# First adjacency over SyncE's and GpSimd's queues, weights folded at earlier steps, the first norm's steps reordered

## The chip, the core and the metric

The kernel runs on one core of one Trainium2 chip. The metric is device time in microseconds (us) of the whole launch; TensorE is PE, VectorE is DVE, ScalarE is ACT, GpSimd is POOL, and SyncE (SP) issues DMAs.

## The reference, cut to what matters

For each of 16 samples there are 1024 nodes of 128 features, `x`, and a weighted adjacency `adj` of 1024 x 1024, all float32.

```python
# stage 0
degree = adj.sum(-1)[:, :, None]
agg = einsum('bid,bij->bjd', x, adj) / degree
x = layernorm(x + relu(concat([x, agg]) @ W.T + b))
# stage 1: four layers; the inputs of the last two are widened by earlier layers
src_agg = einsum('bjv,bij->biv', nodes @ ws + bs, adj / l2norm(adj, rows))
dst_agg = einsum('bjv,bji->biv', nodes @ wd + bd, adj / l2norm(adj, columns))
nodes = tanh(concat([src_agg, nodes @ wn + bn, dst_agg]) @ wu + bu)
# at the end
x = layernorm(x + nodes)
```

## The kernel before, in words

The weights of a layer are folded once (`fold_begin`, `fold_end`, lines 139 to 165): `ws`, `wd` and `wn` are transposed on PE and multiplied by their parts of `wu`, so that a layer needs one product for messages (`pt`, line 484) and one for a node's own part. Folded weights of layers one to three are written to memory (`wsave`, line 165) and fetched layer by layer. The unfolded weights lie in a buffer `raw` that the second sample's adjacency later takes.

The samples are worked one after the other. While a sample goes through its four layers, the adjacency of the next is loaded, squared and summed (`sums`, line 226), scaled and transposed in between. The first sample has no such cover, and its loading, stage 0 and first layer are written out by hand (lines 690 to 934). This is the part that the change touches, besides the last norm.

Adjacency is kept in 8 blocks of 128 rows, each put together from four groups of 32 partitions. `PAIRS` names four pairs of blocks; `load_pair` (line 697) loads one pair with four DMAs of 256 KB, one for each group; `load_nodes` loads half of the nodes. `load_rows` (line 429) loads a quarter of the adjacency once more in another layout, in 8 DMAs of 128 KB, from which DVE's 32 x 32 transposes make the transposed adjacency `at` (`transpose_rows`). Before that, ACT scales the rows by the inverse row norms `rinv` (`scale_rows`, line 438).

Stage 0 of the first sample: each block is squared on ACT (`square`), its degree is reduced on DVE (`degree`), its squares are added up on POOL (`add_square`, seven additions into one), and PE gathers it (`gather`, two matmuls a block). Then come the aggregate scaled by the inverse degree (`scaled`), the product with `W` (`first_weights`), the sum with `x` and the transposing back in PSUM (`with_x`, `with_y`), the norm (`norm_stats` takes statistics on DVE and the power of -0.5 on POOL; half 1 is written by ACT with a shift, half 0 by DVE), and `to_x1`, which transposes the result on PE for the first layer's messages. `row_inverses`, `column_sums` and `inverses` turn the sums of squares into scales.

The first layer is `plain_layer` (line 509): 34 PE steps, and at the steps named in `hooks` work of other engines is put into their queues: scaling of columns (`second0`, `first0`), transposing of rows (`rows0`), folding of the later layers' weights (`folded`), and `sums0`, which makes sums of quarters of the adjacency (`combine`, line 466) for the next layer. The later layers (`aggregate`, line 539) form their products from seven quarter products instead of eight, so they need these sums. Hooks do not set a time: every engine works through its own queue in the order written, and waits by semaphores.

An engine also issues its DMAs in that order. A wait on a DMA's queue holds all that stands behind it in the same engine's queue. The DMAs share eight semaphores in turn for SP and ACT, and eight for POOL, so that the ninth in flight waits until the first has landed.

Of the kernel before, what the change touches and what calls it, by code (L numbers as in the profile page):

```python
# [8 lines left out]
F32 = mybir.dt.float32  # L9
AF = mybir.ActivationFunctionType  # L10
ALU = mybir.AluOpType
# [12 lines left out]
def adj_resnorm_kernel(ctx: ExitStack, tc: tile.TileContext, x, adj, w0, b0, layers, out):  # L24
# [224 lines left out]
    def column_sums(b, state):  # L249

        tr = two.tile([P, N], F32, tag="sq", name=f"acct{b}")
        nc.vector.transpose(tr, state["acc"])
        part = two.tile([P, K], F32, tag="part", name=f"part{b}")
        nc.vector.reduce_sum(part, tr.rearrange("p (k r) -> p k r", r=C), axis=AX.X)
        state["part"] = part
# [113 lines left out]

    def norm_stats(pn, blks, name):  # L370

        n = len(blks)
        stats = one.tile([P, BPH, 6], F32, tag="stats", name=f"st{name}")
        mv = two.tile([P, BPH, 2], F32, tag="mv", name=f"mv{name}")
        for q in range(n):
            nc.vector.bn_stats(stats[:, q], pn[:, blks[q]])
            nc.vector.bn_aggr(mv[:, q], stats[:, q])
        ve = two.tile([P, BPH], F32, tag="ve", name=f"ve{name}")
        nc.vector.tensor_scalar_add(ve[:, :n], mv[:, :n, 1], LN_EPS)
        rstd = two.tile([P, BPH], F32, tag="rst", name=f"rs{name}")  # L380
        nc.gpsimd.tensor_tensor(rstd[:, :n], ve[:, :n], mhalf[:, :n], ALU.pow)
        return mv, rstd

    def norm_write(dst, pn, stats, q):
        mv, rstd = stats
        nc.vector.tensor_scalar(dst, pn, mv[:, q, 0:1], rstd[:, q:q + 1], op0=ALU.subtract, op1=ALU.mult)

    def norm_shift(stats, n, name):
        mv, rstd = stats
        shift = two.tile([P, BPH], F32, tag="shift", name=f"sh{name}")  # L390
        nc.vector.scalar_tensor_tensor(shift[:, :n], mv[:, :n, 0], -1.0, rstd[:, :n], op0=ALU.mult, op1=ALU.mult)
        return shift

    def norm_write_act(dst, pn, stats, shift, q):
        nc.scalar.activation(dst, pn, AF.Identity, bias=shift[:, q:q + 1], scale=stats[1][:, q:q + 1])

# [31 lines left out]

    def load_rows(b, q, st):


        v = adj[b, q * QB * C:(q + 1) * QB * C].rearrange("(k r) (h g j) -> h g r k j", r=C, h=NH, g=G)
        for g in range(G):
            for h in range(NH):
                nc.sync.dma_start(st[g * C:(g + 1) * C, :, h * P:(h + 1) * P], v[h, g])
        return st
# [260 lines left out]
    def load_pair(q, pair, groups):  # L697
        h, k = pair
        for g in groups:
            q.dma_start(a[g * C:(g + 1) * C, h * BPH + k:h * BPH + k + 2], av[h][g, :, k:k + 2])  # L700

    def load_nodes(h):
        for g in range(G):
            nc.sync.dma_start(xn[g * C:(g + 1) * C, h * BPH:(h + 1) * BPH], xv[h][g])

    load_pair(nc.scalar, PAIRS[0], range(G))
    load_nodes(1)
    load_pair(nc.scalar, PAIRS[1], range(2))
    load_pair(nc.sync, PAIRS[1], range(2, G))
    load_nodes(0)  # L710
    load_pair(nc.sync, PAIRS[2], range(G))
    nc.sync.dma_start(w0n, w0)
    nc.sync.dma_start(b0c, b0.rearrange("(p o) -> p o", o=1))
    load_pair(nc.sync, PAIRS[3], range(G))
    raw = Raw()
    wm = message_tile("wm1_0")
    fetched = [fetch_weights(raw, 0, nc.sync, wm)]
    Q = combined(0, "Q")
    rows = {q: load_rows(0, q, Q[i].rearrange("p k (u c) -> p (k u) c", u=2)) for i, q in ((2, 2), (3, 3))}
    fetched += [fetch_weights(raw, l, nc.sync) for l in range(1, NL)]  # L720
    rows[0] = load_rows(0, 0, Q[4].rearrange("p k (u c) -> p (k u) c", u=2))
    rows[1] = load_rows(0, 1, one.tile([P, 2 * NJ, HW // 2], F32, tag="T2", name="rows1_0"))

    make_identity(nc, ident)
    nc.vector.memset(mhalf, -0.5)
# [7 lines left out]
    xT = two.tile([P, N], F32, tag="xT", name="x0_T")  # L733
    for h in (1, 0):
        pt = product(f"xtr0_{h}")
        for q in range(BPH):
            nc.tensor.transpose(pt[:, q * P:(q + 1) * P], xn[:, h * BPH + q], ident)
        nc.scalar.copy(nodes(xT[:, half(h)]), blocks(pt))

    sq = []  # L740
# [25 lines left out]

    for h, k in PAIRS[:-1]:
        for i in range(h * BPH + k, h * BPH + k + 2):
            square(i)
            degree(i)  # L770
            if i != BPH:
                add_square(i)
            for h2 in (1, 0):
                gather(h2, i)
    pt = product("w0tr")
    for k in range(2):
# [33 lines left out]
    degree_row(1)  # L810
    with_x(1)
    with_x(0)
    first, second = 2, 3
# [5 lines left out]
    degree(first)  # L819
    scaled(1)  # L820
    degree(second)
    degree_inverses(0)
    add_square(first)
    nc.vector.tensor_scalar_max(cols[:, :NB], cols[:, :NB], NORM_EPS * NORM_EPS)
    nc.gpsimd.tensor_tensor(inv[:, :NB], cols[:, :NB], mhalf[:, :NB], ALU.pow)
    first_weights(0, 1, xT, agT, yT, blocks, nodes)
    degree_row(0)
    scaled(0)
    with_y(1)
    first_weights(0, 0, xT, agT, yT, blocks, nodes)  # L830
    stats = {1: norm_stats(pn[1], range(BPH), "0_0_1")}
    fold_begin(0, fetched[0], nc.vector.tensor_copy)
    with_y(0)
    fold_end(0, fetched[0])
    rinv = row_inverses(0, inv)
    shift = norm_shift(stats[1], BPH, "0_0_1")
    for q in range(BPH):
        norm_write_act(x1n[:, BPH + q], pn[1][:, q], stats[1], shift, q)
    stats[0] = norm_stats(pn[0], range(BPH), "0_0_0")
    add_square(second)  # L840
    to_x1(1)
    for q in range(BPH):
        norm_write(x1n[:, q], pn[0][:, q], stats[0], q)
    to_x1(0)

# [11 lines left out]
    for b in range(B):  # L857
# [9 lines left out]
        if b == 0:  # L867
            for q in (2, 3):
                scale_rows(rows[q], q, rinv)
            t = messages(b, 0, feats, wm, {0: lambda: column_sums(0, st0)}, with_sums=False)  # L870
            cinv = {}

# [10 lines left out]
            def second0(destination, finish):  # L883
                columns0(range(NJ, NB), 1)
                destination(1, cinv[0])
                columns0(range(NJ), 1)
                for q in (0, 1):
                    scale_rows(rows[q], q, rinv)
# [9 lines left out]
            def sums0(destination, finish):  # L898
                combine_1(y)
                finish(1)  # L900
                combine(2, y, T)
                combine_1(yt)

            def folded(l, part):
                return lambda *_: part(l, fetched[l])

            hooks = {1: lambda *_: inverses(0, st0, NB), 3: rows0, 5: folded(1, fold_begin), 7: cinv0,
                     9: folded(1, fold_end), 10: second0, 18: first0, 19: folded(2, fold_begin),
                     22: folded(2, fold_end), 24: folded(3, fold_begin), 26: sums0, 29: folded(3, fold_end)}
            T = combined(0, "T")  # L910
# [48 lines left out]
        def quarters2(b=b):  # L959
            if b == 0:  # L960
                combine(3, y, T)
                combine(2, yt, Q)
            for i in (3, 4):
                combine(i, yt, Q)
# [5 lines left out]
        if b == 0:  # L970
            hooks[20] = lambda: combine(4, y, T)
        aggregate(b, 1, feats, t, a, at, T, Q, f23, "acc", hooks)
# [104 lines left out]
        else:  # L1077
# [7 lines left out]
            def transpose_last():  # L1085
                pn["last"] = ps_t.tile([P, BPH, P], F32, tag="pt", name="on_1")
                for q in range(BPH):
                    i = BPH + q
                    nc.tensor.transpose(pn["last"][:, q], f4[:, i * P:(i + 1) * P], ident)
                stats[1] = norm_stats(pn["last"], range(BPH), f"1_{b}_1")  # L1090

# [22 lines left out]
    shift = norm_shift(stats[1], BPH, f"1_{b}_1")  # L1114
    for q in range(BPH):
        norm_write_act(o[:, BPH + q], pn["last"][:, q], stats[1], shift, q)
    nc.sync.dma_start(ov[:, BPH:], o[:, BPH:])
    for i in pieces:
        for q in range(2):
            nc.tensor.matmul(pn[i][:, q], f4[:, (i + q) * P:(i + q + 1) * P], ident, start=False, stop=q == 1)  # L1120
        stats[0] = norm_stats(pn[i], range(2), f"1_{b}_0_{i}")
        for q in range(2):
            norm_write(o[:, i + q], pn[i][:, q], stats[0], q)
        nc.sync.dma_start(ov[:, i:i + 2], o[:, i:i + 2])
# [29 lines left out]
```

## Time and profile before

| what | us |
|---|---|
| median of three runs (lowest, highest) | 2563.24 (2561.34, 2564.53) |
| profiled execution, whole | 2558.41 |
| its span, first to last instruction | 2556.6 |
| PE busy in the span | 2524.7 |
| first gather starts | 13.97 |
| gathers end | 31.8 |
| last message product of layer one ends | 49.90 |
| first layer's PE steps end | 89.5 |
| PE's last product before the end | 2548.4 |

A row of the chain of waits or of the timeline gives the start, the duration, the engine, the line in the kernel, the operation and its operands, and how many instructions were merged. A bracket behind it has the time that the engine idled before, and what ended that. A row of waits gives who waited for whom, the total, the number of waits and the longest. A row of the stretches gives each engine's busy time, the granted PE clock, the DMA engines' busy share and GB/s.

### The profile page before, as it was taken

What the parts mean: (1) busy time and instruction counts of PE and PEld (TensorE: products, weight loads), DVE (VectorE), ACT (ScalarE), POOL (GpSimd) and SP (SyncE); (2) the same over time, 40 slices, a digit from 0 to 9 for tenths busy, and PEclk for the clock granted to TensorE, in tenths of its full rate; (3) what the DMA queues carried; (4) which work ended last, traced back from release to release, by engine and by line L of the source; (5) the groups of instructions that cost most, each with busy time, mean ns of one, the idle gap of its engine ahead of it and who ended that gap; (6) DMA issues with size and microseconds to landing.
All of it is one profiled execution on the core that took longest, in us unless ns stands there. A gap on an engine that the chain in (4) does not pass through costs nothing.

```text
span 2556.6 us, 28566 instructions
## 1 busy us (share of the span) xinstructions
PE 2524.7 (99%) x10909; PEld 1197.2 (47%) x10909; DVE 1655.8 (65%) x1982; ACT 836.0 (33%) x1552; POOL 503.3 (20%) x192
## 2 busy tenths in 40 slices
PE   7999999999999999999999999999999999999998
PEld 4453545444454444544445445354543445444453
DVE  5657657576675856657576675765757667585643
ACT  4414324143331423314133241332414333142311
POOL 3311303013030120401213021130301303112000
PEclk9999999999999999999999999999999999999999
DMA  9416345172442715436154361634517245271410
GB/s 187 105 38 126 75 92 98 43 145 56 95 102 49 145 36 99 101 67 126 34 106 99 71 117 42 120 77 92 97 45 141 59 93 105 47 143 40 91 23 9
DMA packets 362313, 219.53 MB, mean 86 GB/s; under 512 B 148929, under 2 KB 333505, under 8 KB 362177
## 3 DMA queue, kind: packets, MB, share of 16 engines
q1 hardware_dynamic: 361696, 216.14, 41.8%
q10 hardware_dynamic: 480, 1.57, 0.3%
q8 instruction: 86, 1.41, 0.2%
q14 instruction: 51, 0.41, 0.1%
HBM read 199.17 MB, written 18.46 MB: 85 GB/s over the span
## 4 chain that ended last, share of the span: by engine, by line
PE 74%; DVE 6%; SPq 6%; DMA 6%; POOL 3%; ACT 3%; issue 1%; POOLq 0%; ACTq 0%; DVEq 0%
PE m L663 28%; PE z L663 22%; PE pt L484 11%; PE pa L411 8%; SPq L225 6%; DMA a<-in_adj_dram 3%; POOL acc L246 2%; DMA out_dram<-y 1%; POOL inv L286 1%; ACT sq L242 1%; PE pw L423 1%; PE pw L422 1%; DVE e L587 1%; PE pa L765 1%; ACT sq L239 1%
## 5 line engine op out<-in xcount | busy, mean ns | idle before, releaser
L363 POOL TENSOR_TENSOR rs<-ve,mhalf 128x32 f32<-128x32 f32 x30 | 162.8, 5428 | 1408.0 <-DVE ve L361 1408.0
L663 PE MATMUL z<-at,t 128*64 128x512 f32 x1224 | 383.7, 592 | 0.0
L663 PE MATMUL m<-Q,S 128*64 128x512 f32 x768 | 339.3, 595 | 2.6 <-ACT e L571 2.6
L663 PE MATMUL m<-T,S 128*64 128x512 f32 x1008 | 292.7, 594 | 0.0
L487 DVE TENSOR_TENSOR t<-pt,wm 128x512 f32<-128x512 f32 x256 | 175.3, 690 | 176.3 <-PE pt L484 176.2
L663 PE MATMUL m<-a,t 128*64 128x512 f32 x1008 | 269.6, 595 | 0.0
L246 POOL TENSOR_TENSOR acc<-acc,sq 128x1024 f32<-128x1024 f32 x90 | 220.4, 2449 | 140.4 <-ACT sq L242 136.9
L663 PE MATMUL z<-a,S 128*64 128x512 f32 x504 | 231.5, 597 | 0.0
L663 PE MATMUL z<-T,t 128*64 128x512 f32 x504 | 228.5, 596 | 2.1 <-DVE T L472 2.1
L663 PE MATMUL z<-a,t 128*64 128x512 f32 x504 | 228.5, 596 | 0.0
L440 ACT ACTIVATE a<-a,rinv 128x256 f32<-128x256 f32 x480 | 198.2, 495 | 51.9 <-DMA a<-in_adj_dram 46.7
L663 PE MATMUL m<-at,t 128*64 128x512 f32 x828 | 214.8, 594 | 0.0
L484 PE MATMUL pt<-wm,f1T 128*128 128x256 f32 x768 | 213.5, 383 | 0.0
L321 DVE TENSOR_TENSOR a<-a,cinv 128x512 f32<-128x512 f32 x250 | 156.6, 698 | 84.5 <-DMA cinv<-dr 82.7
L411 PE MATMUL pa<-a,xn 128*128 128x512 f32 x480 | 210.0, 595 | 0.2 <-DVE e L586 0.2
L663 PE MATMUL z<-at,S 128*64 128x512 f32 x444 | 200.8, 592 | 0.0
L570 ACT COPY e<-m 64x512 f32<-64x512 f32 x63 | 36.7, 582 | 485.7 <-PE m L663 485.3
L663 PEld LDWEIGHTS m<-Q,S 128*64 128x64 f32 x768 | 105.5, 137 | 170.0 <-issue 149.2
L663 PEld LDWEIGHTS z<-at,t 128*64 128x64 f32 x1224 | 120.7, 137 | 130.2 <-issue 111.4
L663 PE MATMUL z<-Q,t 128*64 128x512 f32 x384 | 172.6, 592 | 0.0
L663 PEld LDWEIGHTS m<-T,S 128*64 128x64 f32 x1008 | 102.2, 137 | 145.6 <-issue 124.5
L484 PEld LDWEIGHTS pt<-wm,f1T 128*128 128x128 f32 x768 | 143.3, 190 | 44.0 <-issue 21.6
(189 smaller groups left out, 3723.5 us busy)
## 6 DMA issues: line engine op xcount, KB each, us to landing
a<-in_adj_dram SPq DMA_DIRECT2D x120, 512.0 KB, 12.1
a<-in_adj_dram SPq DMA_DIRECT2D x480, 128.0 KB, 4.0
xn<-in_x_dram SPq DMA_DIRECT2D x128, 64.0 KB, 2.0
wm<-wsave SPq DMA_DIRECT2D x16, 512.0 KB, 3.9
wm<-wsave SPq DMA_DIRECT2D x31, 256.0 KB, 3.3
xs<-in_x_dram SPq DMA_DIRECT2D x60, 128.0 KB, 3.5
cinv<-dr SPq DMA_DIRECT2D x30, 256.0 KB, 5.2
dinv<-dr SPq DMA_DIRECT2D x30, 256.0 KB, 5.0
```

Source lines behind the costliest of these rows:

```text
L225: nc.sync.dma_start(ov[g, :, ks], ys[g * C:(g + 1) * C, ks])
L239: nc.scalar.activation(sq, a[:, i, :], AF.Copy, accum_out=degree)
L242: nc.scalar.activation(sq, a[:, i, :], AF.Square, accum_out=cols[:, i:i + 1])
L246: nc.gpsimd.tensor_add(acc, acc, sq)
L321: engine.tensor_mul(a[:, i, s], a[:, i, s], cinv[:, s])
L363: nc.gpsimd.tensor_tensor(rstd, ve, mhalf[:, :n], ALU.pow)
L411: nc.tensor.matmul(pa, xn[:, i], a[:, i, s], start=(i == 0), stop=(i == NB - 1))
L440: nc.scalar.activation(st[:, k], st[:, k], AF.Copy, scale=rinv[:, q * QB + k:q * QB + k + 1])
L484: nc.tensor.matmul(pt[:, q], f[:, i * P:(i + 1) * P], wm[:, 1 + c], start=(k == 0), stop=(k == nch - 1))
L487: nc.vector.tensor_add(t[j][:, o:o + 2].rearrange("p k a v c -> p k (a v c)"), pt, wm[:, 0][:, None, :].to_broadcast([P, 2, 2 * P]))
L570: nc.scalar.copy(e0[high], A[high])
L663: nc.tensor.matmul(o, x, y, start=start, stop=stop)
```

## The change

Loading: the identity is built first; half 1 of the nodes goes by ACT's queue; of every pair, groups 0 and 1 go by SP's queue and groups 2 and 3 by POOL's; half 0 of the nodes follows the second pair on SP; `w0` and `b0` come behind the four pairs, then all raw weights, then rows 0 and 1, all on SP. Rows 2 and 3 follow the pairs on POOL's queue. ACT issues no adjacency any more.

Stage 0: the transposes of half 0 of the nodes are moved behind the gathers of two pairs; one of the seven additions of squares goes to DVE; the last addition comes before the norm's power on POOL; the node products `with_x` come behind each half's product with `W`; the shift for ACT's writes is made by DVE (times -1) and POOL (times the power); the transposed column sums stand before the norm's writes of half 0; `to_x1(0)`, the reduction of column sums and the scaling of rows 2 and 3 stand behind the first message product.

First layer: folding of layers one to three moves from steps 5, 9, 19, 22, 24, 29 to steps 4, 6, 9, 12, 14, 16; the scaling of rows 0 and 1 moves from step 10 to step 17; `T[3]` is made at step 26 and no longer in the second layer; `T[4]` moves from step 20 to step 12 of the second layer.

Last norm: both pieces' statistics are taken before the first piece is written.

The diff, cut to its core:

```diff
-    def load_rows(b, q, st):
+    def load_rows(b, q, st, queue=nc.sync):
...
-    load_pair(nc.scalar, PAIRS[0], range(G))
-    load_nodes(1)
-    load_pair(nc.scalar, PAIRS[1], range(2))
-    load_pair(nc.sync, PAIRS[1], range(2, G))
-    load_nodes(0)
-    load_pair(nc.sync, PAIRS[2], range(G))
+    make_identity(nc, ident)
+    load_nodes(1, nc.scalar)
+    for p, pair in enumerate(PAIRS):
+        load_pair(nc.sync, pair, range(G // 2))
+        load_pair(nc.gpsimd, pair, range(G // 2, G))
+        if p == 1:
+            load_nodes(0)
     nc.sync.dma_start(w0n, w0)
...
-    load_pair(nc.sync, PAIRS[3], range(G))
...
-    fetched = [fetch_weights(raw, 0, nc.sync, wm)]
+    fetched = [fetch_weights(raw, l, nc.sync, None if l else wm) for l in range(NL)]
...
+    rows = {q: load_rows(0, q, place, nc.gpsimd if i < 2 else nc.sync) for i, (q, place) in enumerate(zip((2, 3, 0, 1), places))}
...
+    nc.vector.tensor_add(sq[6], sq[6], sq[7])
+    add_square(5)
+    add_square(6)
+    to_xT(0)
...
+    add_square(second)
+    degree_row(0)
     first_weights(0, 1, xT, agT, yT, blocks, nodes)
-    degree_row(0)
     scaled(0)
+    with_x(1)
     with_y(1)
     first_weights(0, 0, xT, agT, yT, blocks, nodes)
-    stats = {1: norm_stats(pn[1], range(BPH), "0_0_1")}
+    with_x(0)
+    stats = {1: norm_stats(pn[1], range(BPH), "0_0_1", True)}
...
+            def first_half0():
+                to_x1(0)
+                column_reduce(0, st0, acct)
+                for q in (2, 3):
+                    scale_rows(rows[q], q, rinv)
...
+            def scale0(destination, finish):
                 for q in (0, 1):
                     scale_rows(rows[q], q, rinv)
...
                 combine_1(yt)
+                combine(3, y, T)
...
-            hooks = {1: lambda *_: inverses(0, st0, NB), 3: rows0, 5: folded(1, fold_begin), 7: cinv0,
-                     9: folded(1, fold_end), 10: second0, 18: first0, 19: folded(2, fold_begin),
-                     22: folded(2, fold_end), 24: folded(3, fold_begin), 26: sums0, 29: folded(3, fold_end)}
+            hooks = {1: lambda *_: inverses(0, st0, NB), 3: rows0, 4: folded(1, fold_begin), 6: folded(1, fold_end),
+                     7: cinv0, 9: folded(2, fold_begin), 11: second0, 12: folded(2, fold_end),
+                     14: folded(3, fold_begin), 16: folded(3, fold_end), 17: scale0, 18: first0, 26: sums0}
...
-            hooks[20] = lambda: combine(4, y, T)
+            hooks[12] = lambda: combine(4, y, T)
```

More of the change, by code (lines that the diff above doesn't have):

```diff
@@ L249, in column_sums, with column_transpose, column_reduce @@
     def column_sums(b, state):
+        column_reduce(b, state, column_transpose(b, state))
+    def column_transpose(b, state):
         tr = two.tile([P, N], F32, tag="sq", name=f"acct{b}")
         nc.vector.transpose(tr, state["acc"])
+        return tr
+    def column_reduce(b, state, tr):
         part = two.tile([P, K], F32, tag="part", name=f"part{b}")
@@ L368, in norm_end, with norm_stats @@
         nc.vector.tensor_mul(ys[:, ks], ys[:, ks], rstd[:, :, None].to_broadcast([P, n, C]))
-    def norm_stats(pn, blks, name):
+    def norm_stats(pn, blks, name, shifted=False):
         n = len(blks)
@@ L380, in norm_stats, with norm_write_act @@
         rstd = two.tile([P, BPH], F32, tag="rst", name=f"rs{name}")
+        shift = None
+        if shifted:
+            shift = two.tile([P, BPH], F32, tag="shift", name=f"sh{name}")
+            nc.vector.tensor_scalar_mul(shift[:, :n], mv[:, :n, 0], -1.0)
         nc.gpsimd.tensor_tensor(rstd[:, :n], ve[:, :n], mhalf[:, :n], ALU.pow)
-        return mv, rstd
+        if shifted:
+            nc.gpsimd.tensor_mul(shift[:, :n], shift[:, :n], rstd[:, :n])
+        return mv, rstd, shift
     def norm_write(dst, pn, stats, q):
-        mv, rstd = stats
+        mv, rstd, _ = stats
         nc.vector.tensor_scalar(dst, pn, mv[:, q, 0:1], rstd[:, q:q + 1], op0=ALU.subtract, op1=ALU.mult)
[L388 to L395, printed above, removed]
+    def norm_write_act(dst, pn, stats, q):
+        _, rstd, shift = stats
+        nc.scalar.activation(dst, pn, AF.Identity, bias=shift[:, q:q + 1], scale=rstd[:, q:q + 1])
     def summed(name):
@@ L434, in load_rows @@
             for h in range(NH):
-                nc.sync.dma_start(st[g * C:(g + 1) * C, :, h * P:(h + 1) * P], v[h, g])
+                queue.dma_start(st[g * C:(g + 1) * C, :, h * P:(h + 1) * P], v[h, g])
         return st
@@ L700, in load_pair, with load_nodes @@
             q.dma_start(a[g * C:(g + 1) * C, h * BPH + k:h * BPH + k + 2], av[h][g, :, k:k + 2])
-    def load_nodes(h):
+    def load_nodes(h, q=nc.sync):
         for g in range(G):
-            nc.sync.dma_start(xn[g * C:(g + 1) * C, h * BPH:(h + 1) * BPH], xv[h][g])
-    load_pair(nc.scalar, PAIRS[0], range(G))
-    load_nodes(1)
-    load_pair(nc.scalar, PAIRS[1], range(2))
-    load_pair(nc.sync, PAIRS[1], range(2, G))
-    load_nodes(0)
-    load_pair(nc.sync, PAIRS[2], range(G))
+            q.dma_start(xn[g * C:(g + 1) * C, h * BPH:(h + 1) * BPH], xv[h][g])
+    make_identity(nc, ident)
[5 more added lines that the diff above has]
+            load_nodes(0)
     nc.sync.dma_start(w0n, w0)
     nc.sync.dma_start(b0c, b0.rearrange("(p o) -> p o", o=1))
-    load_pair(nc.sync, PAIRS[3], range(G))
     raw = Raw()
     wm = message_tile("wm1_0")
-    fetched = [fetch_weights(raw, 0, nc.sync, wm)]
+    fetched = [fetch_weights(raw, l, nc.sync, None if l else wm) for l in range(NL)]
     Q = combined(0, "Q")
[L719 to L724, printed above, removed]
+    places = [Q[i].rearrange("p k (u c) -> p (k u) c", u=2) for i in (2, 3, 4)]
+    places.append(one.tile([P, 2 * NJ, HW // 2], F32, tag="T2", name="rows1_0"))
+    rows = {q: load_rows(0, q, place, nc.gpsimd if i < 2 else nc.sync) for i, (q, place) in enumerate(zip((2, 3, 0, 1), places))}
     nc.vector.memset(mhalf, -0.5)
@@ L733, in adj_resnorm_kernel, with to_xT @@
     xT = two.tile([P, N], F32, tag="xT", name="x0_T")
-    for h in (1, 0):
+    def to_xT(h):
         pt = product(f"xtr0_{h}")
@@ L738, in adj_resnorm_kernel @@
         nc.scalar.copy(nodes(xT[:, half(h)]), blocks(pt))
+    to_xT(1)
     sq = []
@@ L765, in gather, with squares_of @@
         nc.tensor.matmul(pa[h], xn[:, i], a[:, i, half(h)], start=(i == BPH), stop=(i == BPH - 1))
-    for h, k in PAIRS[:-1]:
+    def squares_of(h, k):
         for i in range(h * BPH + k, h * BPH + k + 2):
@@ L770, in adj_resnorm_kernel, with gathers_of @@
             degree(i)
-            if i != BPH:
-                add_square(i)
+    def gathers_of(h, k):
+        for i in range(h * BPH + k, h * BPH + k + 2):
             for h2 in (1, 0):
                 gather(h2, i)
+    for pair in PAIRS[:2]:
+        squares_of(*pair)
+        gathers_of(*pair)
+    nc.vector.tensor_add(sq[6], sq[6], sq[7])
+    add_square(5)
+    add_square(6)
+    to_xT(0)
     pt = product("w0tr")
@@ L810, in adj_resnorm_kernel @@
     degree_row(1)
-    with_x(1)
-    with_x(0)
+    squares_of(*PAIRS[2])
+    gathers_of(*PAIRS[2])
+    add_square(0)
+    add_square(1)
     first, second = 2, 3
@@ L819, in adj_resnorm_kernel @@
     degree(first)
-    scaled(1)
     degree(second)
     degree_inverses(0)
+    scaled(1)
     add_square(first)
@@ L834, in adj_resnorm_kernel @@
     fold_end(0, fetched[0])
+    for q in range(BPH):
+        norm_write_act(x1n[:, BPH + q], pn[1][:, q], stats[1], q)
+    stats[0] = norm_stats(pn[0], range(BPH), "0_0_0")
     rinv = row_inverses(0, inv)
[L836 to L840, printed above, removed]
+    acct = column_transpose(0, st0)
     to_x1(1)
@@ L843, in adj_resnorm_kernel @@
         norm_write(x1n[:, q], pn[0][:, q], stats[0], q)
-    to_x1(0)
     kept = scratch.tile([N, D], F32, tag="kept", name="kept0")
@@ L867, in adj_resnorm_kernel @@
         if b == 0:
-            for q in (2, 3):
-                scale_rows(rows[q], q, rinv)
-            t = messages(b, 0, feats, wm, {0: lambda: column_sums(0, st0)}, with_sums=False)
+            def first_half0():
[3 more added lines that the diff above has]
+                    scale_rows(rows[q], q, rinv)
+            t = messages(b, 0, feats, wm, {0: first_half0}, with_sums=False)
             cinv = {}
@@ L959, in quarters2 @@
         def quarters2(b=b):
[L960 to L963, printed above, removed]
+            for i in ((2, 3, 4) if b == 0 else (3, 4)):
                 combine(i, yt, Q)
@@ L1089, in transpose_last @@
                     nc.tensor.transpose(pn["last"][:, q], f4[:, i * P:(i + 1) * P], ident)
-                stats[1] = norm_stats(pn["last"], range(BPH), f"1_{b}_1")
+                stats[1] = norm_stats(pn["last"], range(BPH), f"1_{b}_1", True)
             hooks = {30: residual_last, 31: transpose_last}
@@ L1113, in adj_resnorm_kernel @@
             nc.tensor.matmul(pn[i][:, q], x1v[:, (i + q) * P:(i + q + 1) * P], ident, start=q == 0, stop=False)
-    shift = norm_shift(stats[1], BPH, f"1_{b}_1")
     for q in range(BPH):
-        norm_write_act(o[:, BPH + q], pn["last"][:, q], stats[1], shift, q)
+        norm_write_act(o[:, BPH + q], pn["last"][:, q], stats[1], q)
     nc.sync.dma_start(ov[:, BPH:], o[:, BPH:])
+    stats = {}
     for i in pieces:
@@ L1120, in adj_resnorm_kernel @@
             nc.tensor.matmul(pn[i][:, q], f4[:, (i + q) * P:(i + q + 1) * P], ident, start=False, stop=q == 1)
-        stats[0] = norm_stats(pn[i], range(2), f"1_{b}_0_{i}")
+        stats[i] = norm_stats(pn[i], range(2), f"1_{b}_0_{i}")
+    for i in pieces:
         for q in range(2):
-            norm_write(o[:, i + q], pn[i][:, q], stats[0], q)
+            norm_write(o[:, i + q], pn[i][:, q], stats[i], q)
         nc.sync.dma_start(ov[:, i:i + 2], o[:, i:i + 2])
```

## The prediction

> **What bounds the kernel now.** I read the page's busy shares first, then who TensorE (PE) waited for, then the DMA rate and the granted clock by stretches, then the instructions in order of time on the queues that the change moves.
>
> ```profile
> PE 2524.7 (99%) x10909; PEld 1197.2 (47%) x10909; DVE 1655.8 (65%) x1982; ACT 836.0 (33%) x1552; POOL 503.3 (20%) x192
> ```
>
> PE is busy in 2524.7 of 2556.6 us: 31.9 us at most are to be had without removing matmuls, and the change removes none. So I ask where PE is idle.
>
> ```profile
> PE xtr L737 <- DMA xn<-in_x_dram: 12.0, 2, 8.1
> PE m L663 <- ACT e L571: 2.6, 1, 2.6
> PE z L663 <- DVE T L472: 2.1, 1, 2.1
> PE x1tr L807 <- DVE x1n L386: 1.5, 1, 1.5
> PE x1tr L807 <- ACT x1n L395: 0.8, 1, 0.8
> ```
>
> 12.0 us lie before the first gather (start at 13.97 us), 2.3 in the first norm (41 to 44 us), 4.7 in the second message layer (111 and 121 us). The chain ends PE's last message product of layer one at 49.90 us; I call that moment E. The rest of the idle time is mostly the last 8 us.
>
> ```profile
> 0.00:13.00 13.00, 1.09 (x4) 0.71 (x4) 3.31 (x8) 0.90 (x1) 0.76 (x7) 1.00 0.93 185
> 13.00:26.00 13.00, 12.91 (x30) 6.21 (x31) 4.83 (x7) 8.02 (x15) 8.80 (x4) 1.00 1.06 211
> 112.70:116.00 3.30, 3.30 (x10) 0.98 (x8) 1.27 (x2) 3.22 (x7) 1.02 (x2) 0.50 0.00 0
> 122.90:126.20 3.30, 3.30 (x9) 0.85 (x11) 3.17 (x4) 1.30 (x3) 2.03 (x1) 0.50 0.00 0
> ```
>
> The last three columns are clock, DMA share and GB/s. Until 26 us the DMA engines are full at 209 to 214 GB/s, with one queue or two. After each of the late stalls PE ran 3.4 us at half clock, so a stall of 2.6 us costs 2.6 + 1.7.
>
> ```profile
> 26.28 7.99 SPq L435 DMA_DIRECT2D Q<-in_adj_dram  x16
> 16.96 4.81 POOL L755 TENSOR_TENSOR sq<-sq,sq 128x1024 f32<-128x1024 f32 x2 [15.60 <-ACT sq L752]
> 32.33 1.65 POOL L825 TENSOR_TENSOR inv<-cols,mhalf 128x8 f32<-128x8 f32 x1 [0.82 <-DVE cols L824]
> 37.46 1.01 POOL L381 TENSOR_TENSOR rs<-ve,mhalf 128x4 f32<-128x4 f32 x1 [3.48 <-DVE ve L379]
> 64.06 3.29 ACT L440 ACTIVATE rows<-rows,rinv 128x256 f32<-128x256 f32 x8
> 69.83 2.32 DVE L445 STREAM_TRANSPOSE at<-rows 128x1024 f32<-128x1024 f32 x2
> 81.02 2.29 DVE L468 TENSOR_TENSOR T<-a 128x2048 f32<-128x2048 f32 x1
> ```
>
> POOL today issues no DMA; its additions (2.4 us each) run from 17 us on and the norm's pow at 37.46 finds it free. These are the prices below.
>
> **What the Trainium skill says.** "SBUF — State Buffer", Door 1: partitions 0 to 31 reach 8 of 16 DMA ports, and 189 GB/s in 1 MiB; 64 and up reach the other 8. The 209 GB/s of 32-partition loads agree. Same page, "Can I just issue two DMAs to hit both halves?": two concurrent transfers to opposite halves gave only 6% more. No stretch here has opposite halves side by side for long, so the trace is silent. "DMA: Bandwidth & Descriptors", SWDGE vs HWDGE: a DMA issued by GpSimd has its descriptors built in software on GpSimd itself, with about 1 us to the first byte. The trace before has none. "TensorE: Matmul & The Clock Gate", Part 1: an idle window of about 3.4 us halves the clock; the two 0.50 rows agree.
>
> **The change part by part.**
>
> *POOL's queue.* It now issues 8 pair DMAs (2.10 MB) and 16 row DMAs (2.10 MB) ahead of all its arithmetic. In the built program the ninth waits until the first has landed, and so on to the 24th, which waits for the 16th. So POOL's first addition cannot start before 3.15 MB have landed by its queue. Call that time F. SP moves as much meanwhile (its half, nodes, weights), ACT 0.26: 6.55 MB. At 213 GB/s plus the skill's 6%, 226, from 2 us: 31; landing and last issue 1.5: F = 32.5. Bounds: if both halves add up, 3.15 MB at 190 from 3 us, plus landing and issue: F = 21. From issue alone: 1.3 us for the identity, 24 issues at 0.5 (SP's row above) give 13, at 1.0 (the skill) 25, at 2.0 for the 16 row DMAs, four times the pieces of a pair, 41. I take 1.0, so landing decides, and keep 21 and 41.
>
> *POOL's chain after F.* Five additions 12.1, pow for the rows 1.65, the last addition 2.4 (moved ahead of the norm's pow; before it came after), pow 1.0, the new multiplication for the shift about 0.8 (no row; 0.2 to 1.0, a small pow), gaps 0.3: F + 18.3. Before, five additions were done by 31.5, in DMA's shadow. One addition goes to DVE (about 1.2, hidden: DVE is idle there). Then ACT writes four blocks 1.5, transpose and copy 1.1, products of block 2 1.2, the transposes of half 0 0.6 (now behind the first product), three products 3.6 at the half-clock rate of before (4.86 for four). E = F + 26 = 58.5.
>
> *Loads and PE.* PE no longer needs half 0 of the nodes first, so gathers of two pairs start near 9 instead of 13.97. But the transposes of w0 stand in PE's order before the third pair, and w0 is now issued on SP behind all four pairs: 2.49 MB by SP, about 26 us. PE then needs w0 and a factor row 1.0 and eight gathers' passes 6.9: gathers end near 34 against 31.8, with the two node products (1.7) still to come. From there weights, norm, products: 15, so 50 by PE's path. POOL's path (58.5) is later; this part costs nothing by itself and gains nothing. Its cover is POOL; if POOL were early, PE's 50 would leave E unchanged at this DMA rate.
>
> *Shift on POOL, split of column sums, x1 of half 0 behind the first product.* They take DVE steps (0.15 and 2.5) off the norm's way; worth the 2.3 us of norm waits at most, contained in E above.
>
> *Weights folded sooner.* PE's fold work (8.4 us) moves from steps 5 to 29 to steps 4 to 16 of layer one. Gain: the last weights are saved some 12 us sooner, so the second sample's adjacency, whose landing now holds ACT's square at 101 us and through ACT's order the reads of m, is there in time; T[4] is at hook 12 instead of 20. The 2.6 and 2.1 us stalls go with both half-clock spells: -8.1 (4.7 + 3.4). Late next: DVE. Rows 0 and 1 are scaled at step 17, behind the folds on ACT: let step 18 start at S, the folds end at S - 1.7, ACT scales until S + 5.5 (2 x 3.3), DVE transposes the last rows until S + 7.9. DVE then has dest 0.7, columns 1.3, subtraction 2.3, e 0.7, three subtractions (T[3] is new among them) 6.9, e 0.7: S + 20.4, tanh 0.7 makes S + 21.1. PE, without folds in these 16 steps, is through steps and two products at S + 13.8 + 1.9 = S + 15.6. Before, folds of 6 us and an earlier scaling covered this. New stall 5.0 to 5.5 plus half clock 1.7: +6.7. Folds net: -1.4.
>
> *Tail.* Both pieces' statistics now precede the writes: one pow with its way (0.7 + 0.15) is hidden: -0.85. Nothing in between changes.
>
> **Sum.** E moves by F + 26 - 49.9; with -1.4 and -0.85, the change is F - 26.2. For F = 32.5: +6.3. The profiled execution took 2558.41 (span 2556.6 and 1.8 around it), 4.8 below the median of 2563.24; the difference is carried onto the median: 2569.5, say 2570.
>
> **Rivals.**
>
> *A, forecast (0.42):* as above. For it: 211 GB/s with one queue, 214 with two, and the skill's 6%. Against it: those two queues mostly wrote the same half.
>
> *B, partial adding up (0.23):* the two queues reach about 265 GB/s; 6.55 MB take 25 us, F = 28, +1.8: 2565. The change then does in sum nothing.
>
> *C, faster (0.23):* the split by partition halves (0 to 63 on SP, 64 to 127 on POOL) doubles the ports; F = 21, -5.2, 2558. It decides from F below 21 to 22. It also holds if F is near 26 and the DVE stall of 5 us doesn't come, as ACT's order might be slacker than I see. For it: the skill's port table. Against: its own measurement of two transfers, and POOL's 24 issues, which must each stay under 0.8 us.
>
> *D, slow issue (0.12):* 2 us for a row DMA on POOL: F = 41, +15, 2578; more is possible.
>
> **How the numbers follow.** About 0.2% (5.1 us) is what a measurement of this kernel can tell from no change. A lies above it three times in four (F over 31.3), else within; B within, one in ten each outside; C below it four in five; D above. Faster: 0.02 + 0.19 = 0.21. Slower: 0.32 + 0.02 + 0.12 = 0.46. Same: 0.33. The range leaves out the best third of C and the worst half of D: 2556 to 2583. A alone: 2565 to 2575.
>
> **What would show it.** Right: POOL's first addition after 30 us, the shift after 48, PE idle about ten us before the first message product and about five at the end of layer one (waiting for tanh of half 0), no wait for e or T[4] afterwards. Wrong: a DMA rate well above 230 GB/s before 20 us, POOL adding by 22 us, or no DVE wait at the layer's end; then C. Issues of over 1.5 us on POOL's queue mean D.

## The result, and the profile after

The changed kernel takes 2572.86 us in the median of four runs (2568.34 to 2574.69), the kernel before 2563.02 (four runs now, where the table above had three); the ratio is 1.0036, with a 95% interval of 1.0019 to 1.0053. The change costs 9.8 us. The forecast was 2570 and slower.

The profiled execution of the changed kernel (2574.69, span 2572.9) was the longest of its four, that of before (2558.41) lay 4.6 below its median. So the two profiles differ by 16.3. From the start of the third layer to the end of the span, nearly all of it the same code, the 14 profiles of this study need 2428.6 to 2437.3 us without a relation that I can find to what was edited; before has the shortest. I therefore compare traces up to the start of the third layer, and medians for the whole.

The page's busy shares come first, then the waits of PE (total, number, longest).

```profile
PE 2526.1 (98%) x10909; PEld 1196.9 (47%) x10909; DVE 1658.4 (64%) x1983; ACT 835.7 (32%) x1552; POOL 518.2 (20%) x217
```

```profile
PE xtr L744 <- DMA xn<-in_x_dram: 12.7, 1, 12.7
PE w0tr L795 <- DMA w0n<-in_L_gnn_W_dram: 9.5, 1, 9.5
PE pt L492 <- ACT f1T L684: 5.0, 1, 5.0
PE rp L301 <- DVE sp L297: 1.5, 1, 1.5
PE m L671 <- DVE t L510: 0.8, 1, 0.8
PE pt L492 <- ACT x_T L826: 0.7, 1, 0.7
```

PE's work is what it was; POOL has 25 instructions more. The waits for `e` and `T` in the second layer and for the norm in stage 0 (2.3 us) are gone. But stage 0 has two new ones, 1.5 us for `rp` and 0.7 us for x1: the change puts the row inverses (`row_inverses`, whose product on PE is `rp`) behind the statistics of half 0 on DVE, ahead of which they stood before. The wait for tanh of half 0 (`f1T`) is there with the forecast 5.0 us. The largest new wait was not forecast: 9.5 us for `w0`. The chain of waits (start, duration, what) goes through it:

```profile
14.36 17.96 DMA w0n<-in_L_gnn_W_dram
...
32.36 0.69 PE w0tr L795 x2
33.05 0.85 PE dinv L275 x4
33.90 8.86 PE pa L774 x16
...
55.03 2.07 PE pt L492 x4
57.11 0.85 PE x1tr L825 x4
57.96 2.80 PE pt L492 x12
```

`w0` is issued at 14.36 and lands 17.96 us later; only then does PE gather the last two pairs. E, the end of the last message product of layer one, is 60.76. In the kernel before, the last line of the same kind ends at 49.90:

```profile
45.04 4.86 PE pt L484 x16
```

In POOL's timeline the queue is shorter than forecast:

```profile
1.52 4.39 POOL L708 DMA_DIRECT2D a<-in_adj_dram  x8 [0.20 <-issue]
9.25 0.60 POOL L443 DMA_DIRECT2D Q<-in_adj_dram  x1 [3.34 <-DMA a<-in_adj_dram]
...
29.27 4.78 POOL L764 TENSOR_TENSOR sq<-sq,sq 128x1024 f32<-128x1024 f32 x2
...
49.98 0.20 POOL L394 TENSOR_TENSOR sh<-sh,rs 128x4 f32<-128x4 f32 x1
```

The ninth DMA waits until an earlier one has landed, as forecast; each issue takes 0.5 to 0.6 us of POOL. The first addition (F) starts at 29.27. In the stretches (after the busy times: clock, DMA share, GB/s) two partition halves at once give 239 and 206 GB/s, against 211 from 13 to 26 us of the kernel before: at best a little faster, far from double. The last two rows show half clock during the wait for `w0` and behind the wait for `f1T`:

```profile
12.00:16.00 4.00, 3.29 (x7) 1.92 (x8) 3.41 (x4) 2.17 (x4) 1.78 (x4) 1.00 1.07 239
16.00:20.00 4.00, 4.00 (x9) 1.81 (x8) 2.17 (x3) 2.58 (x6) 1.51 (x3) 1.00 1.07 206
28.00:32.00 4.00, 0.00 (x0) 0.00 (x0) 2.17 (x3) 0.00 (x0) 3.48 (x5) 0.50 1.10 207
107.00:111.00 4.00, 3.98 (x10) 2.79 (x12) 1.26 (x3) 3.94 (x7) 0.00 (x0) 0.50 0.64 124
```

At the end of layer one, ACT's and DVE's timelines show the late scaling and the added subtraction:

```profile
88.55 3.30 ACT L448 ACTIVATE rows<-rows,rinv 128x256 f32<-128x256 f32 x8
103.33 2.29 DVE L478 TENSOR_TENSOR T<-T,a 128x2048 f32<-128x2048 f32 x1
105.53 0.68 DVE L538 TENSOR_TENSOR e<-e,z 128x512 f32<-128x512 f32 x1
```

### The profile page after: what moved, and what is told of

The parts are those of the page before. It is cut to its first block, busy times and chain, and to the rows that moved or that the text cites. A ratio compares the mean times of both kernels' runs of the same rounds, so it can differ in the third digit from the quotient of the medians.

```text
span 2572.9 us, 28596 instructions
## 1 busy us (share of the span) xinstructions
PE 2526.1 (98%) x10909; PEld 1196.9 (47%) x10909; DVE 1658.4 (64%) x1983; ACT 835.7 (32%) x1552; POOL 518.2 (20%) x217
## 3 DMA queue, kind: packets, MB, share of 16 engines
q0 software_dynamic: 1408, 4.20, 0.8%
## 4 chain that ended last, share of the span: by engine, by line
PE 64%; DVE 10%; DMA 9%; SPq 8%; POOL 4%; ACT 4%; issue 1%; ACTq 0%; DVEq 0%; POOLq 0%
PE m L671 24%; PE z L671 17%; PE pt L492 10%; PE pa L419 8%; SPq L225 7%; DMA a<-in_adj_dram 4%; POOL acc L246 2%; DMA out_dram<-y 2%; POOL inv L292 1%; DVE a L327 1%; ACT sq L242 1%; DVE e L595 1%; PE pw L430 1%; PE pw L431 1%; DMA cinv<-dr 1%
```

## The experiments

First theory: `w0` is late because SP's queue moves small pieces beside POOL's large ones; PE waits for it, and that sets E. Rival: POOL's long queue and late additions set E, and `w0` has cover. Third: the split of the loads over halves of the partitions. For the layers: the folds gain in layer two what they lose at the end of layer one.

| run | ratio to before (95%) | medians, us | w0 used at | E | third layer starts |
|---|---|---|---|---|---|
| before | 1 | 0 | 25.96 | 49.90 | 128.05 |
| changed kernel | 1.0036 (1.0019, 1.0053) | +9.8 | 32.36 | 60.76 | 139.46 |
| p_tail | 0.9996 (0.9988, 1.0005) | -0.8 | | 51.31 | 129.50 |
| p_hooks | 1.0003 (0.9994, 1.0011) | +0.7 | | 49.89 | 128.59 |
| p_start | 1.0036 (1.0023, 1.0048) | +8.9 | 32.02 | 58.59 | 135.22 |
| e_w0 | 1.0013 (1.0007, 1.0020) | +3.6 | 22.92 | 55.41 | 134.10 |
| e_rows | 1.0001 (0.9993, 1.0010) | -0.2 | 25.27 | 49.94 | 128.63 |
| e_both | 0.9992 (0.9984, 1.0000) | -2.3 | 20.27 | 46.25 | 124.96 |
| e_node | 1.0026 (1.0018, 1.0033) | +6.3 | 29.48 | 55.59 | 134.30 |
| n_hooks | 0.9974 (0.9965, 0.9983) | -7.5 | | 50.75 | 120.33 |
| p_T3 | 0.9999 (0.9991, 1.0008) | +0.5 | | 51.04 | 124.02 |
| best | 0.9965 (0.9952, 0.9977) | -8.8 | 19.95 | 47.15 | 116.73 |
| best2 | 0.9971 (0.9961, 0.9982) | -7.3 | 22.78 | 48.34 | 117.92 |
| best3 | 0.9954 (0.9941, 0.9968) | -11.3 | | 47.39 | 116.97 |

Kernels with the loading of before have E from 49.89 to 51.31, so a single E is good to about 1.4 us. The changed kernel and p_start, which are alike up to E, even lie 2.2 us apart.

### The three parts by themselves

p_tail is the kernel before with the last norm's new order:

```diff
-        stats[0] = norm_stats(pn[i], range(2), f"1_{b}_0_{i}")
+        stats[i] = norm_stats(pn[i], range(2), f"1_{b}_0_{i}")
+    for i in pieces:
         for q in range(2):
-            norm_write(o[:, i + q], pn[i][:, q], stats[0], q)
+            norm_write(o[:, i + q], pn[i][:, q], stats[i], q)
```

> The kernel before with the last norm's change alone. Marks: from the last statistics' start (2548.38 us in the profile before) to the end of the span 8.2 us before, 6.8 us in the changed kernel. Theory (one pow with its way is hidden): 6.8 to 7.4 here, time -0.85 to -1.4. Rival (the last store's landing hides it): 8.2, time unchanged. Either is inside what the median can tell, so the mark decides.

p_hooks is the kernel before with the first layer's part (steps of the folds, rows 0 and 1 scaled at step 17, `T[3]` in layer one, `T[4]` at step 12):

```diff
+            hooks = {1: lambda *_: inverses(0, st0, NB), 3: rows0, 4: folded(1, fold_begin), 6: folded(1, fold_end),
+                     7: cinv0, 9: folded(2, fold_begin), 11: second0, 12: folded(2, fold_end),
+                     14: folded(3, fold_begin), 16: folded(3, fold_end), 17: scale0, 18: first0, 26: sums0}
```

> The kernel before with the first layer's part alone (folds at steps 4 to 16, scaling at step 17, T[3] at step 26, T[4] at step 12). Theory (both late stalls with their half-clock spells go, -8.2, and a new wait for tanh of half 0 comes at the end of layer one, 5.0 plus half clock 1.7 plus 0.8 for a DVE step): the third layer's message products start within 1 us of 128.1, time -1 to +1, E unchanged at 49.9. Rival 1 (the new wait is a child of the late start, not of the order on DVE): no wait for f1T, start at 120, time -8. Rival 2 (the folds also delay the loads): later than 131, time over +3.

p_start is the changed kernel with both of these as before, so the loading and stage 0 alone (with the last norm's shift left on POOL, where the changed kernel also computes it):

```diff
+            hooks = {1: lambda *_: inverses(0, st0, NB), 3: rows0, 5: folded(1, fold_begin), 7: cinv0,
+                     9: folded(1, fold_end), 10: second0, 18: first0, 19: folded(2, fold_begin),
+                     22: folded(2, fold_end), 24: folded(3, fold_begin), 26: sums0, 29: folded(3, fold_end)}
```

> The changed kernel with layer one's hooks and the last norm as before: loading and stage 0 alone. Theory (all of the loss is made before E, and nothing later gives any of it back): E near 60.8, third layer's message products start 10.9 later than 128.1, near 139, time +10 to +12. Rival (a late start is partly absorbed, since the weights and rows are there earlier for the steps of layer one): start at 134 or sooner, time under +6.

p_start alone has the whole loss, +8.9; the other two are within what can be measured. From the start of the first piece's statistics to the end of the span p_tail needs 6.8 us, the kernel before 8.2: 1.4 less, more than the forecast 0.85, because the first piece's write (0.73) now lies beside the second piece's pow too.

p_hooks shows both halves of the forecast, the new wait in full and most of the gain. The one long wait of PE after E is

```profile
PE pt L484 <- ACT f1T L676: 5.0, 1, 5.0
```

The second layer's messages end 50.04 after E instead of 43.11 (+6.9), and from there the third layer starts after 28.66 us instead of 35.04 (-6.4). Part of why layer two gains is in SP's timeline. In the kernel before the second sample's adjacency is issued at

```profile
88.30 3.89 SPq L186 DMA_DIRECT2D a<-in_adj_dram  x8
```

and in p_hooks, where the folded weights are saved sooner, at

```profile
77.63 3.95 SPq L186 DMA_DIRECT2D a<-in_adj_dram  x8
```

so ACT's squares, with the reads of `m` behind them, no longer stand before data that has not landed: ACT's wait of 10.2 us for this adjacency in the kernel before is absent in p_hooks. The wait for `T` (2.1 us before) went with `T[4]` made at step 12 instead of 20; p_hooks makes both moves, and no run takes them apart.

### w0 or POOL?

e_w0 moves `w0` and `b0` to ACT's queue:

```diff
     load_nodes(1, nc.scalar)
+    nc.scalar.dma_start(w0n, w0)
+    nc.scalar.dma_start(b0c, b0.rearrange("(p o) -> p o", o=1))
...
-    nc.sync.dma_start(w0n, w0)
-    nc.sync.dma_start(b0c, b0.rearrange("(p o) -> p o", o=1))
```

> The changed kernel with w0 and b0 loaded by ACT's queue right behind half 1 of the nodes. Theory 1 (PE's path: PE stood 9.5 us before the transposes of w0, and the third pair's gathers behind them): w0 is there by 18, gathers end near 35 instead of 42.8, then POOL's chain (first addition 29.3, plus 26) decides: E near 55, time 5 to 6 below the changed kernel. Theory 2 (POOL's queue decides alone): E stays at 60 or more, time within 1 of the changed kernel. Theory 3 (POOL doesn't matter): E near 52, time 8 to 9 below.

The time falls by 5.6 us of the changed kernel's 9.2 (1.0036 of this comparison's before): `w0` did set E. What remains shows POOL in its timeline beside DVE's. DVE has the norm's shift ready at 41.42, and POOL, still adding squares, takes up the pow at 44.34:

```profile
41.26 0.16 DVE L391 TENSOR_SCALAR sh<-mv 128x4 f32<-128x4 f32 x1
44.34 1.01 POOL L392 TENSOR_TENSOR rs<-ve,mhalf 128x4 f32<-128x4 f32 x1
```

F is 28.32 and E is F + 27.1, where the forecast had F + 26. The gathers end at 35.30, since the last pairs land late (2.6 us of waits).

e_rows leaves `w0` where the change put it and takes the 2.1 MB of rows off POOL's queue; they go by SP's, behind the first layer's weights and ahead of the later layers':

```diff
-    rows = {q: load_rows(0, q, place, nc.gpsimd if i < 2 else nc.sync) for i, (q, place) in enumerate(zip((2, 3, 0, 1), places))}
+    rows = {q: load_rows(0, q, place) for q, place in zip((2, 3), places)}
+    fetched += [fetch_weights(raw, l, nc.sync) for l in range(1, NL)]
+    rows.update({q: load_rows(0, q, place) for q, place in zip((0, 1), places[2:])})
```

> The changed kernel, but rows 2 and 3 go by SP's queue, behind the first layer's weights, as in the kernel before; POOL issues the 8 pair transfers only. First theory (w0 lands late because SP's queue gets a small share beside POOL's 4.2 MB, and PE waits for w0): 2.1 MB less stand beside SP's queue, w0 lands near 24 us instead of 32.3, gathers end near 35, E near 50, and the time is 7 to 10 us under the changed kernel's. Second theory (POOL's long queue and late additions alone set E; w0 has cover): POOL adds from about 20 us and the time falls by the same 7 to 10, but w0 still lands after 30. Third (the split of the loads over two queues is not what costs): within 2 us of the changed kernel.

The loss is gone, with `w0` in use at 25.27 after a wait of 2.6 us instead of 9.5, as in the first theory:

```profile
PE w0tr L797 <- DMA w0n<-in_L_gnn_W_dram: 2.6, 1, 2.6
```

The pairs still go by two queues, so the third theory has no part. e_both has both edits:

> The changed kernel with both: w0 and b0 on ACT's queue behind half 1 of the nodes, rows 2 and 3 on SP's queue. If the additions on POOL (28.3 to 44.3 us in the run with w0 alone moved) and the late landing of the last pairs are what is left of the loss in that run, E falls from 55.4 to 47 to 50 and the time is 4 to 7 us under that run, 2557 to 2561. If POOL's queue has no part in it, the time stays at that run's 2564.

E falls to 46.25, below the 47 to 50 expected, and the time to 2.3 under before (0 to 4.1). So the rows on POOL's queue cost on two paths: through `w0` (moving it gains 5.6 with rows on POOL, 2.1 without) and through POOL's additions and the last pairs. The reordered steps of stage 0 are in all of these runs; what they are worth by themselves was not run.

### Why SP's queue was slow

In the changed kernel's DMA view from 13 to 19 us, q0 is POOL's queue and q1 SP's:

```profile
DMA packets 707, 1.30 MB, mean 217 GB/s; under 512 B 116, under 2 KB 429, under 8 KB 707
q0 software_dynamic: 353, 1.14, 90.1%
q1 hardware_dynamic: 354, 0.16, 15.9%
```

353 packets against 354, but 1.14 MB against 0.16. (116 of the 707 are records of under 512 bytes.) By the trace's packet records POOL's data packets have 4096 bytes and SP's at this time, half 0 of the nodes, 512. It looks as if the queues took turns packet by packet. The Trainium skill has a rule of this kind ("DMA: Bandwidth & Descriptors", Queues, rings and completion order: each engine goes round its queues at packet granularity); I had read past it. Its packet is a bundle of descriptors, and whether the trace's records are such packets is not shown. Nor do even counts hold everywhere: from 28 to 33 us, where SP's queue moves `w0` in pieces of 1024 bytes and weights in pieces of 512, the same trace counts 913 packets of SP's queue (0.43 MB) against 232 of POOL's (0.62 MB). So the trace shows that SP's queue got an eighth of the bytes while it moved the nodes; the turns by packets are a likely reason, not a shown one. e_node tests it by putting half 0 of the nodes on ACT's queue:

```diff
-        if p == 1:
-            load_nodes(0)
...
     load_nodes(1, nc.scalar)
+    load_nodes(0, nc.scalar)
```

> The changed kernel with half 0 of the nodes on ACT's queue, behind half 1, so that SP's queue holds pieces of 4096 bytes only until w0. If it is the pieces of 512 bytes that kept SP's queue at 25 to 30 GB/s beside POOL's for 10 us, SP's pairs keep up with POOL's, w0 lands by 26 us, and the time is 4 to 6 us under the changed kernel's, near that of the run with w0 moved. If POOL's queue takes more than its half whatever the pieces, w0 lands after 30 us and the time stays within 2 us of the changed kernel.

Neither outcome came: `w0` at 29.48, the time about 3 us under the changed kernel's. From 13 to 19 us SP's and POOL's queues, both with pieces of 4096 bytes, are even in packets and nearly in bytes, and ACT's small pieces (q10) have about as many packets:

```profile
DMA packets 661, 1.61 MB, mean 268 GB/s; under 512 B 109, under 2 KB 291, under 8 KB 661
q1 hardware_dynamic: 227, 0.73, 49.3%
q0 software_dynamic: 227, 0.78, 48.1%
q10 hardware_dynamic: 207, 0.09, 8.1%
```

But SP's queue was empty from 6 to 12 us, because SP itself waited (its waits until 20 us; L708 are the pairs, L720 is `w0`):

```profile
SPq L708 <- DMA xn<-in_x_dram: 9.6, 5, 4.7
SPq L720 <- DMA xn<-in_x_dram: 3.7, 1, 3.7
```

SP and ACT take eight semaphores in turn. ACT's eight slow node transfers held them, and SP could issue its later pairs and `w0` only as these landed. So with large pieces SP's queue keeps up where it has work, but the time was lost again to the semaphores. The changed kernel has such waits too, if shorter:

```profile
SPq L708 <- DMA xn<-in_x_dram: 4.4, 1, 4.4
SPq L712 <- DMA xn<-in_x_dram: 4.1, 3, 2.1
```

They are a rival cause of its late `w0`, which SP issues only at 14.36. In e_rows SP waits as long (4.2 and 4.1) and issues `w0` at 14.19, and yet `w0` is there at 25.27; so the 7 us between the two come after the issue, from the rows on POOL's queue. How much the small pieces and the semaphores each add before that is not separated. best2 ran into the same (SP's eight pair issues are spread from 0.74 to 20.54 us).

### The end of layer one

n_hooks is the kernel before with folds one and two as changed, rows 0 and 1 scaled right behind fold two, fold three at steps 20 and 22, `T[3]` left in layer two, `T[4]` at its step 12:

```diff
+            def fold_and_scale(destination, finish):
+                fold_end(2, fetched[2])
+                for q in (0, 1):
+                    scale_rows(rows[q], q, rinv)
...
+                     7: cinv0, 9: folded(2, fold_begin), 11: second0, 12: fold_and_scale, 18: first0,
+                     20: folded(3, fold_begin), 22: folded(3, fold_end), 26: sums0}
```

> The kernel before with the weights folded sooner as in the changed kernel for layers one and two, layer three at steps 20 and 22, rows 0 and 1 scaled behind fold two at step 12 (not at 17), T[3] left in the second layer, T[4] at its step 12. If the new wait for tanh of half 0 at the end of layer one comes from the scaling at step 17 and the T[3] moved ahead of it, it is gone here, and so are the waits for e and T of the second layer: 6 to 8 us under the kernel before. If removing one wait only brings the next, the time is within 2 us of the kernel before.

7.5 us under before: no wait for `f1T`, none for `e` or `T`; the third layer starts 69.58 after E instead of 78.15. Inside the third layer there are two small new waits, 0.8 us for column sums and

```profile
PE pt L484 <- ACT f23T L676: 1.3, 1, 1.3
```

p_T3 is p_hooks with only `T[3]` put back:

```diff
                 combine_1(yt)
-                combine(3, y, T)
...
         def quarters2(b=b):
+            if b == 0:
+                combine(3, y, T)
```

> The kernel before with the first layer's part of the change, but T[3] made in the second layer as before. By the sum in the prediction DVE is 2.3 us less late at the end of layer one: the wait for tanh of half 0 falls from 5.0 to about 2.7, the second layer's messages end 47 to 48 after E instead of 50.04, and the time is 1.5 to 3 us under the run with the whole part. If T[3] only moves the wait, the second layer waits for T[3] or T[4] and the time is the same.

The waits of PE in p_T3:

```profile
PE pt L484 <- ACT f23T L676: 3.2, 1, 3.2
PE pt L484 <- ACT f1T L676: 2.8, 1, 2.8
```

The wait for `f1T` falls by 2.2 as the sum said, but the work moves on into DVE's queue in layer two, and PE then waits 3.2 us at the start of layer three. The median is as before: a wait displaced, not removed. n_hooks, which also scales the rows earlier, has only the 1.3 us.

### A version that beats both

best joins e_both's loading, n_hooks and the new last norm; best2 puts half 0 of the nodes behind `w0` on ACT's queue; best3 is best with `T[2]` and `T[3]` in gaps of DVE in layer one:

```diff
                 combine_1(y)
-                finish(1)
                 combine(2, y, T)
+                finish(1)
+                combine(3, y, T)
                 combine_1(yt)
```

> Everything that helped, together: loading and stage 0 as in the run with w0 on ACT's queue and rows on SP's (E 46.25, 3.65 before the kernel before), folds and scaling as in the run that saved 7.5 us (third layer 69.6 after E), last norm as changed. If the gains add, the third layer starts at 115.8 us instead of 128.05 and the end of the span gains 1.4: 12 to 14 us under the kernel before. If the earlier start only brings the next wait (the load of the second sample's adjacency, or DVE at the end of layer one), 7 to 9 us.

> As the combined version, with half 0 of the nodes on ACT's queue behind w0, so that SP's and POOL's queues hold only the pairs' pieces of 4096 bytes until the last pair. If nodes of 512-byte pieces on SP's queue held the third pair back (PE waited 1.1 us for it), SP's part of the pairs keeps up and E falls by another 1 to 2 us. If ACT's small pieces share with the pairs just as SP's did, E stays within 0.5 us, or PE waits for half 0 of the nodes instead.

> The combined version, with T[2] made ahead of the first half's tanh in layer one and T[3] right behind it, where DVE idled 2.97 and 1.78 us, and no longer in the second layer. If DVE's queue in the second layer is what makes PE wait 1.30 us for f23T there, that wait goes, no wait for f1T comes, the third layer starts 69.6 after E as before, and the time falls by about 1.3 us against the combined version, to 9 to 11 us under the kernel before. If DVE was late at the end of layer one by then, a wait for f1T of 0.3 to 1 us comes instead and the time is the same.

best gains 8.8, less than the 12 to 14 expected: E came at 47.15, not 46.25, and the wait for `f23T` of 1.3 us stays; the rest of the gap lies within its interval (5.9 to 12.3). In best2 E is later (48.34), PE waits 2.0 us for a pair, and the time is no better. In best3 the wait for `f23T` is gone and none for `f1T` came; it is 11.3 us under before (8.2 to 15.1) and has the lowest median of this study. That it beats best is shown by the missing wait only, since the two intervals overlap.

## Why the prediction was right or wrong

**Time and sign: right, by a sum in which terms of different sign failed.** Forecast +6.3, measured +9.8. That the number came so near is luck.

**The step that failed** is "Loads and PE": `w0` behind the pairs, "2.49 MB by SP, about 26 us", and so a path of 50 us on PE that "costs nothing by itself" under POOL's 58.5. The order on SP's queue was listed, the size of the delay was wrong: 26 us comes out only if SP's queue gets half of the rate (2.49 MB at 113 GB/s from 2 us, plus landing), and from 13 to 19 us it got 0.16 of 1.30 MB. The start was wrong too: the first gather came at 13.59, not near 9, because half 1 of the nodes on ACT's queue landed at 12.57. `w0` came at 32.36 (+6.4), `w0` and the factor row took 1.5 instead of 1.0, the eight gathers' passes 8.86 instead of 6.9 behind the long wait (+2.0), E came 18.0 after the gathers instead of 16.7 (+1.3, and the new wait of 1.5 us for `rp` lies in this stretch). PE's path became 60.8 and set the end. e_w0 shows that it did.

**POOL's queue: mechanism right, F too late.** F was 29.27, not 32.5. The issue of a row's DMA took 0.58 us, not the 1.0 that I took after the skill's page; the page's 1 us ("DMA: Bandwidth & Descriptors", Specifications) is the time to the first byte, not POOL's time for an issue. Landing decided, as assumed. With the measured F, POOL's path is F + 26 = 55.3; in e_w0, where it comes into view, E is F + 27.1. By POOL alone the kernel would have lost 3.1 us by the forecast's sum (an estimate); the forecast came near because 3.2 us too many here stand against 5.5 not seen there.

**The DMA rate: right.** I took 226 GB/s from the skill's +6% for two halves ("SBUF — State Buffer", Can I just issue two DMAs to hit both halves?). The changed kernel has 204 to 254 in stretches of 4 us from 4 to 32 us, and 268 in e_node with equal packets on both halves, against 203 to 218 of before until 24 us. So more than 6% in the stretches where both move large packets, and in no stretch the double rate that case C needed. C fell, and so did D (issues of 2 us).

**Folds: both terms in place, net +0.6 in the trace (+0.7 in the median of p_hooks), forecast -1.4.** At the end of layer one +6.9 against 6.7, though the sum for ACT was 0.6 us too long (S - 1.7 and two scalings of 3.3 make S + 4.9, not S + 5.5). In layer two -6.4 against -8.1: a wait of 0.6 us for `t` is new, and the half clock of the boundary reaches into layer two.

**Shift and split of the column sums:** the 2.3 us of norm waits are gone, but 1.5 us for `rp` and 0.7 us for x1 came, so that by PE's waits next to nothing was gained. The forecast did not have the wait for `rp`. **Tail:** -1.4, not -0.85.

**Sum as measured:** E +10.9, folds +0.6, tail -1.4: +10.0 for 9.8. That it fits so well is in part chance: with p_start's E, 58.59, the sum would be +7.9.

## What to carry to other kernels

When transfers of several queues overlap, do not share out the bytes equally: here a queue of 512-byte pieces beside one of 4096 got an eighth of the bytes. What stood behind the small pieces arrived late, and moving `w0` to another queue took 5.6 us off. Look also at the semaphores: a queue whose engine waits for one has nothing to send. A path that a forecast calls covered needs the same care as the one that covers it, above all where it stands or falls with one landing. Work moved earlier pays only if what it displaces has a gap to fall into; look for the gap in the queue of the engine that does it, as best3 did.

## What the runs showed that I had not expected

- Even packets and uneven bytes: 353 against 354 packets in 6 us, at 1.14 against 0.16 MB; later in the same trace the packets are uneven as well (232 of POOL's queue against 913 of SP's).
- POOL issues a DMA of 256 KB in 0.55 us (eight in 4.39) and one of 128 KB in rows' layout in 0.58 us, though the latter has four times as many pieces. The profile's page counts 1408 packets for the 4.20 MB; the rows' 2.1 MB in pieces of 512 bytes would alone be 4096, so on POOL's queue several pieces count as one packet. The same rows on SP's queue, in e_rows, count as packets of 512 bytes.
- A wait of 2.1 to 2.8 us does not always halve the clock. In the kernel before, waits of 2.6 and 2.1 us each did; in p_tail the same wait of 2.64 us, and in p_T3 one of 2.75, left it at 1.00; in p_start 2.75 us halved it and 2.15 did not. The skill ("TensorE: Matmul & The Clock Gate", Part 1) says that an idle window of about 3.4 us halves the clock and that the window runs freely. The second fits, since waits of one length end differently; the first does not, since 2.1 us was enough here, and the measurement decides. My 1.7 us for each wait is thus an upper price for these short waits.
